# A decoder layer on one core: feed-forward tiles in the gates' order, quantisation spread over two feature tiles, a first unit in groups of three half steps, and own PSUM banks for two projection pieces

## The chip, the core and the metric

The kernel runs on one core of one Trainium2 chip. The metric is the device time of one execution in microseconds (us). The engines are TensorE (PE in the profile; PEld is its loading of weights), VectorE (DVE), ScalarE (ACT), GpSimd (POOL) and SyncE (SP), which issues most of the DMAs. Each of the four compute engines works through its own instructions in order.

## What is computed

Everything is float32. The batch has 4 sequences of 1024 tokens with 512 features. The reference, cut to what matters:

```python
# attention: 32 heads of 16 channels; every projection is two linear layers in a row
q, k, v = (lin(lin(x, w, wb), vw, vb) for each of q, k, v)
o = softmax(q @ k.T / 4) @ v                  # per head, 1024 x 1024 scores
x = layernorm(x + lin(shuffled(o), wo))
# gates: x is taken as (1024 channels, 512 positions); halves h and c, z0 prepended
out = ctx + conv1d(h, weight, kernel 2) + bias    # 2048 output channels
i, o, g, f = split(out, 4)
c = sigmoid(f) * c_before + sigmoid(i) * tanh(g)
x = layernorm(x + concat(sigmoid(o) * tanh(c), c))
# feed-forward: quantised activations, ternary weight
x_dq = clip(round(x / scale), -127, 127) * scale
x = layernorm(x + x_dq @ (ternary_weight - 1).T + bias)
```

## The kernel before

**Set-up (attention, L311-L369).** The two linear layers of q, of k and of v are folded into one weight each. For q and k this takes 16 matmuls of 128 x 128 by 128 x 512 apiece (L358-L363), accumulated in four PSUM banks each and copied out by VectorE (tiles 1 and 3) and ScalarE (tiles 2 and 4) at L364-L368. The pool of these banks has eight one-bank buffers; the first goes to ten matmuls of zeros (`idle`), the next eight to the two folds. At L369 the pool is closed, and at L371 and L372 the attention's two pools are opened: `ps_st` with four one-bank buffers and `ps_nat` with two two-bank buffers, eight banks in all.

**Pieces.** `project` (L393) makes 160 or 176 columns of q or k for eight heads: 16 matmuls of 32 output columns, four of them side by side (`by_quarters`, L53). `qk_pieces` (L427) is the list of six such pieces. `fold_v` (L408), `project_v` (L414) and `out_piece` (L436) are pieces of the same shape for the folding of v, for v and for the projection of the attention's output. Each takes one buffer of `ps_st`.

**Units.** A unit is a sequence and a group of four heads, 32 units in all. `nat` (L444) multiplies q by k for two heads in order to find each row's maximum (a VectorE reduction, L473, or L469 for single tiles); each head uses 32 of the 128 rows of TensorE's array, and `pair` says which two of the four row groups. `scores` (L510) makes the transposed scores for two heads, whose exponentials ScalarE takes (L538); `weigh` (L543) multiplies them by v. In the usual unit the `nat` of the next unit and the `scores` of this one go side by side, 32 half steps per unit (L682). The two ends differ (L648-L680): ahead of the first unit (`u == -1`) there is only `nat`, in 16 steps of two half steps each, the second with two single `ps_st` tiles (`apart`) instead of a `ps_nat` tile; between the steps 25 pieces are spread evenly (the last three of v's fold, six of q, sixteen of v). In the last unit there is only `scores`, with one `out_piece` behind every even step while any is left, which is until step 10. Behind it, one last `weigh` and the start of the second sequence's normalisation close the attention (L725-L736).

**Tail.** Sequences go in two rounds, (0, 2) and then (1, 3). A round has 32 gates: for each of four feature tiles t, for each of the two sequences, for each of four gates g (L987-L990). The conv with two taps is computed for three outputs at a time with four matmul groups per gate (`gate`, L793, L798-L803); the inputs `xf` of these groups are sums and differences made by VectorE (`fir_parts`, L172, L185-L191). VectorE adds each gate's results to the context in four operations (L807, L810, L811, L813), and ScalarE applies the sigmoid or tanh (L814). `pc` and `pa` are the PSUM tiles, two buffers each. After the fourth gate `combine` (L822) makes two token tiles, t and 4 + t, on GpSimd and ScalarE, their statistics (`third`, L842), the square root (`fourth`, L117), the normalisation (`fifth`, L121) and a sum on GpSimd (`sixth`, L856).

`feed_forward` (L922) goes over the 16 token tiles of the round's two sequences. `quantise` (L867) is one ScalarE operation (L871) and two of VectorE (L872, L873); `turn` (L876) transposes on TensorE and copies back on ScalarE (L881); `feed` (L884) multiplies in one of two PSUM buffers, and `residual` (L890) adds and takes statistics (L892, L893). A tile is quantised four tiles ahead; the first four are quantised in the gates, and the first two are turned between the taps of one of the last gates.

**What sets the order.** The order is written by hand. `after(n, work)` (L758) puts work into a list that is due n steps later, and `step()` (L761), called after every gate and every feed-forward tile, issues what is due on whichever engine it needs. The offsets of `combine` are these (L859), for second, third, fourth, fifth and sixth:

```python
        steps = (4, 6, 7, 8, 9) if last else (1, 3, 4, 5, 6)
```

and the order of the feed-forward tiles and the places of quantisation (`place` counts 0 to 7 in the last feature tile alone, L992) are

```python
    order = [t for t in range(NT) if t % 4 < 3] + [3, 7]
...
                    if place in (1, 2, 3, 4):
                        quantise(batches[0], order[place - 1])
```

Of the kernel before, what the change touches and what calls it, by code (L numbers as in the profile page):

```python
# [8 lines left out]
F32 = mybir.dt.float32  # L9
# [3 lines left out]
PSUM = bass.MemoryType.PSUM  # L13

P = 128
# [232 lines left out]
def attention(ctx, tc, a, attn_d, ident, shared, hand):  # L248
# [73 lines left out]
    pt = ps.tile([P, P], F32, tag="ps", name="idle_ps")  # L322
    for n in range(10):
        nc.tensor.matmul(pt, idle, idle, start=True, stop=True)
    for which, (w, v, dst) in enumerate((("wq", "vq", b_q), ("wk", "vk", b_k), ("wv", "vv", None))):
# [38 lines left out]
        for f in range(FT):  # L364
            if f % 2:
                nc.scalar.copy(w_d[:, f, :], pts[f])  # L366
            else:
                nc.vector.tensor_copy(w_d[:, f, :], pts[f])  # L368
    setup_ps.close()  # L369

    ps_st = ctx.enter_context(tc.tile_pool(name="ps_st", bufs=4, space=PSUM))  # L371
    ps_nat = ctx.enter_context(tc.tile_pool(name="ps_nat", bufs=2, space=PSUM))  # L372

    units = [(b, g) for b in range(B) for g in range(NG)]
    NU = len(units)
    QW = 256
# [13 lines left out]

    late_rows = []

    def project(p, which, t0, n, packed):  # L393

        b, gg = divmod(p, 4)
        w, bias = ((w_q, b_q), (w_k, b_k))[which]
        cols = slice(t0, t0 + n)
        pt = ps_st.tile([P, QW], F32, tag="st", name=f"proj{p}_{which}_{t0}")
        by_quarters(nc, pt[:, 0:n], lambda f: w[:, f, gg * P : (gg + 1) * P], lambda f: xts[b][:, f, cols])
        nc.scalar.activation(packed[:, cols], pt[:, 0:n], AF.Identity, bias=bias[:, gg : gg + 1], scale=1.0)  # L400
        if t0 + n == S:
            to_quadrants(2 * p, which, packed)
            if which == 0 and p > 0:
                late_rows.append(lambda: to_quadrants(2 * p + 1, 0, packed))
            else:
                to_quadrants(2 * p + 1, which, packed)

    def fold_v(f, half):  # L408
        cols = slice(half * QW, half * QW + QW)
# [4 lines left out]
    def project_v(b, t, half):  # L414
# [12 lines left out]
    def qk_pieces(p, which):  # L427


        parts = [(0, 176), (176, 176), (352, 176), (528, 176), (704, 160), (864, 160)]  # L430
        return [lambda part=part: project(p, which, *part, packs[:, which, :]) for part in parts]

    def v_pieces(b, t):
        return [lambda half=half: project_v(b, t, half) for half in range(2)]
# [197 lines left out]
    for u in range(-1, NU):  # L632
        fill = []
        if (u + 3) % 2 == 0 and (u + 3) // 2 < NU // 2:
            fill += qk_pieces((u + 3) // 2, 0)
        elif u % 2 == 0 and u // 2 + 1 < NU // 2:
            fill += qk_pieces(u // 2 + 1, 1)
        if u == -1:
            fill = folds[5:] + fill
            fill += [piece for t in range(NT) for piece in v_pieces(0, t)]  # L640
        elif units[u][0] + 1 < B:
            fill += v_pieces(units[u][0] + 1, units[u][1])
        if u == -1:
# [4 lines left out]
        if u == -1 or u + 1 == NU:  # L648
            total, done = len(fill), 0
            for i in range(HS // 2):  # L650
                if u == -1:
                    after = [nat(0, i, 0), nat(0, i, 1, apart=True)]
                else:
                    after = [scores(u, i, i % 2), scores(u, i, 1 - i % 2, wide=True)]
                for work in after:
                    work()
                if i % 2 == 0 and weighing:
                    weigh(*weighing.pop(0))
                if u >= 0 and i % 2 == 1:
# [3 lines left out]
                if u >= 0 and i > 1 and firsts:  # L663
                    firsts.pop(0)()
                if i == 1 and u >= 0:
                    hand.first_w = hand.load_conv(0, None)
                if i in (3, 5) and u >= 0:
                    hand.load_ctx(i // 2 - 1)
                if i in (8, 9, 10, 11) and u >= 0:
                    hand.sum_taps(hand.first_w, i - 8)  # L670
                if i < 2 and u >= 0:
                    shift(u, 1, i == 0)
                if i in (8, 10) and u == -1:
                    shift(0, 0, i == 8)
                if i in (2, 5, 8, 11) and stages:
                    stages.pop(0)()
                until = total * (i + 1) // (HS // 2)
                for piece in fill[done:until]:
                    piece()
                done = until  # L680
        else:
            for h in range(HS):  # L682
                i, half = divmod(h, 2)
                for work in (nat(u + 1, i, half), scores(u, i, 1 - half)):
                    work()
                if h % 4 == 1 and weighing:
                    weigh(*weighing.pop(0))
                if h in (1, 3):
                    shift(u, 1, h == 1)
                if h in (17, 19):  # L690
                    shift(u + 1, 0, h == 17)
                if h == 2 and late_rows:
                    late_rows.pop()()
                if h % 4 == 3:
                    weighing.append((u, h // 4))
                    if fill:
                        fill.pop(0)()
                    elif u > 24 or u == 24 and h > 24:
                        out_pieces.pop(0)()
                if h in (5, 9, 13, 20) and stages:  # L700
                    stages.pop(0)()
                if h == 5 and u == 24:
                    hand.load_w_o()
                    hand.load_attention(0, big_slot(0, "big0"))
                    hand.load_residual(0)
                    hand.load_rest()
                if h == 21 and 25 <= u < 29:
                    hand.prepare_w_f(u - 25)
                if h == 21 and u == 29:
                    hand.prepare_rest()  # L710
                if h == 5 and u == 30:
                    hand.x1[0], firsts = hand.first_norm(0)
                    firsts.pop(0)()
                    hand.xf[0], parts = hand.fir_parts(0, hand.x1[0], shared)
                    firsts.extend(parts)
                if h == 5 and u == 29:
# [22 lines left out]
def tail(ctx, tc, a, out, ident, eps, hand):  # L739
# [18 lines left out]
    def after(steps, work):  # L758
        later.append((now + max(steps, 1), work))
# [59 lines left out]
            scale=1.0,  # L819
        )  # L820

    def combine(b, t, k, last):  # L822


        u, y, x = us[b, t], ys2[b], x1[b]
# [228 lines left out]
```

## Time and profile before

| what | us |
|---|---|
| median of three runs (2443.67 to 2444.45) | 2444.41 |
| the profiled execution | 2444.41 |
| its span, first to last instruction | 2442.6 |
| set-up and first pieces, to 56.7 | 56.7 |
| ahead of the first unit, 56.7 to 117.7 | 61.0 |
| the usual units, 117.7 to 1909 | 1791.3 |
| last unit, to 1951 | 42.0 |
| first round: 32 gates to 2104.2, feed-forward to 2166.8 | 153.2, 62.6 |
| projection of the second round, to 2222 | 55.2 |
| second round: gates to 2373.7, feed-forward and end to 2442.6 | 151.7, 68.9 |

The granted TensorE clock is 0.999 of full speed over the span. A row of the timeline gives start, duration, engine, line and operation, `out<-in`, shapes and count; in brackets stands how long the engine was idle before it and who ended that idle time. A row of waits gives the waiting line, the releaser, and total, number and longest of such waits. One float32 matmul of the program is two matmul instructions in the trace. Matmuls are pipelined, so that the durations of neighbours overlap: what one costs is the distance from its start to the next one's.

### The profile page before, as it was taken

To read this page: it belongs to the slowest core of one execution; us is meant where nothing else is said; L and a number is where in the kernel's file an instruction comes from. 1 tells how busy PE (TensorE), PEld (TensorE's weight loads), DVE (VectorE), ACT (ScalarE), POOL (GpSimd) and SP (SyncE) were. 2 spreads that over 40 slices of the span, in tenths; PEclk is the share of its full clock that TensorE was granted. 3 is DMA by queue.
4 is the path that set the end of the run, shared out by engine and by line. 5 is a ranking of instruction groups with operands and counts; after the bars stand their busy time and mean duration, and the time that the engine had idled before them with its cause. 6 is when DMAs were issued, how large, how long until landed. Compare 5 with 4: busy or idle time off the path is not lost.

```text
span 2442.6 us, 74358 instructions
## 1 busy us (share of the span) xinstructions
PE 2426.3 (99%) x32604; PEld 1692.5 (69%) x32604; DVE 1740.9 (71%) x2181; ACT 1337.1 (55%) x2592; POOL 374.2 (15%) x310
## 2 busy tenths in 40 slices
PE   9999999999999999999999999999999999999998
PEld 5566666666666666666666666666666699647994
DVE  3777777777777777777777777777777476878677
ACT  1066666666666666666666666666655723411342
POOL 2000000000000000000000000200020268322761
PEclk9999999999999999999999999999999999999999
DMA  6101112111111111011111114111120242160301
GB/s 220 50 12 21 21 21 60 21 21 22 24 22 25 30 47 25 19 23 22 21 21 24 23 21 129 27 25 22 26 84 12 81 148 94 61 225 18 121 35 69
DMA packets 80852, 121.70 MB, mean 50 GB/s; under 512 B 39072, under 2 KB 39328, under 8 KB 80528
## 3 DMA queue, kind: packets, MB, share of 16 engines
q1 hardware_dynamic: 79808, 115.77, 17.3%
q8 instruction: 256, 4.19, 0.8%
q10 hardware_dynamic: 720, 1.18, 0.1%
q14 instruction: 68, 0.56, 0.1%
HBM read 80.77 MB, written 18.35 MB: 41 GB/s over the span
## 4 chain that ended last, share of the span: by engine, by line
PE 97%; DVE 2%; ACT 1%; issue 0%; DMA 0%; SPq 0%; DVEq 0%; ACTq 0%
PE nat L457 22%; PE av L553 20%; PE st L527 18%; PE proj L59 10%; PE pc L803 5%; PE pa L803 5%; PE v L59 5%; PE pf L887 4%; PE po L59 2%; PE po L237 2%; PE fold L361 1%; PE fold L59 1%; PE tr L879 1%; DVE u L813 0%; DVE y L121 0%
## 5 line engine op out<-in xcount | busy, mean ns | idle before, releaser
L473 DVE TENSOR_REDUCE mx<-nat 128x2 f32<-128x1024 f32 x1008 | 1187.6, 1219 | 439.0 <-PE st L527 412.0
L538 ACT ACTIVATE at<-st 128x512 f32<-128x512 f32 x2016 | 1042.3, 603 | 607.7 <-PE st L527 595.3
L457 PE MATMUL nat<-qk 32*128 32x512 f32 x4032 | 1012.5, 614 | 0.5 <-DVE mx L473 0.5
L527 PE MATMUL st<-qk 32*128 32x256 f32 x8064 | 997.8, 388 | 0.0
L527 PEld LDWEIGHTS st<-qk 32*128 32x128 f32 x8064 | 663.1, 184 | 44.9 <-issue 3.7
L553 PE MATMUL av<-at,v_sb 128*32 128x256 f32 x8192 | 498.5, 382 | 1.5 <-ACT at L538 1.5
L457 PEld LDWEIGHTS nat<-qk 32*128 32x128 f32 x4032 | 343.7, 184 | 188.2 <-DVE mx L473 119.7
L553 PEld LDWEIGHTS av<-at,v_sb 128*32 128x32 f32 x8192 | 241.4, 110 | 223.1 <-ACT at L538 92.2
L600 POOL TENSOR_TENSOR o_n<-o_sb,rbc 128x512 f32<-128x512 f32 x64 | 97.1, 1538 | 1672.4 <-DMA rbc<-rec_d 1488.0
L59 PE MATMUL proj<-xT,w_qk 128*32 128x176 f32 (+1 forms) x6144 | 259.4, 311 | 0.7 <-ACT w_qk L366 0.7
L59 PEld LDWEIGHTS proj<-xT,w_qk 128*32 128x32 f32 x6144 | 181.7, 110 | 81.5 <-ACT at L538 59.9
L803 PE MATMUL pc<-xf,w 128*128 128x171 f32 x1024 | 160.1, 308 | 4.6 <-DVE u L807 4.0
L803 PE MATMUL pa<-xf,w 128*128 128x171 f32 x1024 | 159.8, 308 | 0.0
L803 PEld LDWEIGHTS pc<-xf,w 128*128 128x128 f32 x1024 | 151.9, 189 | 6.3 <-DVE u L807 4.8
L803 PEld LDWEIGHTS pa<-xf,w 128*128 128x128 f32 x1024 | 152.1, 189 | 0.0
L814 ACT ACTIVATE u<-u,b_c 128x512 f32<-128x512 f32 x64 | 46.3, 723 | 167.3 <-DVE u L813 166.3
L59 PE MATMUL v<-w_v,xT 128*32 128x256 f32 x2048 | 122.5, 382 | 0.0
L887 PE MATMUL pf<-w_f,xq_t 128*128 128x512 f32 (+1 forms) x264 | 115.2, 581 | 1.7 <-ACT xq_t L881 1.7
L566 DVE TENSOR_TENSOR o_sb<-av,o_sb 128x256 f32<-128x256 f32 x128 | 54.3, 424 | 71.5 <-PE av L553 70.9
L59 PEld LDWEIGHTS v<-w_v,xT 128*32 128x32 f32 x2048 | 60.8, 110 | 58.0 <-ACT at L538 16.5
L170 POOL TENSOR_TENSOR w<-w 128x512 f32<-128x512 f32 x64 | 81.0, 1298 | 100.3 <-DMA w<-in_conv_wT 56.6
L564 ACT COPY o_sb<-av 128x256 f32<-128x256 f32 x128 | 48.0, 375 | 77.9 <-PE av L553 59.3
(99 smaller groups left out, 1325.7 us busy)
## 6 DMA issues: line engine op xcount, KB each, us to landing
qk<-qk SPq DMA_DIRECT2D x256, 64.0 KB
w<-in_conv_wT SPq DMA_DIRECT2D x32, 512.0 KB
u<-in_ctx SPq DMA_DIRECT2D x16, 1024.0 KB
xT<-in_xT SPq DMA_DIRECT2D x16, 512.0 KB
rbc<-rec_d SPq DMA_DIRECT2D x128, 64.0 KB
attn<-o_n SPq DMA_DIRECT2D x256, 32.0 KB
big<-attn SPq DMA_DIRECT2D x4, 2048.0 KB
y<-in_x SPq DMA_DIRECT2D x4, 2048.0 KB
```

Of the source, the lines that this page charges most:

```text
L59: nc.tensor.matmul(pt[r, :], lhsT(f)[:, r], rhs(f), start=f == 0, stop=f == FT - 1)
L170: self.nc.gpsimd.tensor_tensor(w[:, i, tap, :], w[:, i, 0, :], w[:, i, 1, :], op)
L237: nc.tensor.matmul(pt, attn_t[:, f, t * P : (t + 1) * P], self.w_o[:, f, cols], start=f == 0, stop=f == FT - 1)
L457: nc.tensor.matmul(pts[n], q_ts[u % 4][r : r + 32, qt * P : (qt + 1) * P], k_ts[u % 4][r : r + 32, kh * 512 : kh * 512 + 512], start=True, ...
L473: nc.vector.tensor_reduce(mxs[u][:, qt, 2 * pair : 2 * pair + 2, kh], pt, AX.X, ALU.max, negate=True)
L527: nc.tensor.matmul(st[:, k * QW : k * QW + QW], k_ts[u % 4][r : r + 32, kt * P : (kt + 1) * P], q_ts[u % 4][r : r + 32, qq * QW : qq * QW ...
L538: nc.scalar.activation(at, st, AF.Exp, scale=0.25)
L553: nc.tensor.matmul(av[32 * j : 32 * j + 32, :], v_sb[b % 2][:, kt, c * VW : c * VW + 32], ats[u, 2 * i + n // 2, j][:, n % 2 * QW : n % 2 ...
L566: nc.vector.tensor_add(o, av, o)
L600: nc.gpsimd.tensor_mul(o_n[:, :, half * 256 : half * 256 + 256], o_sb[:, cols].rearrange("p (s e) -> p e s", e=2), rbc[:, cols].rearrange( ...
L803: nc.tensor.matmul(pt, w[:, i, tap, o : o + P], xf[:, tap, i, :], start=i == 0, stop=i == FT - 1)
L887: nc.tensor.matmul(pt, xq_ts[b, t][:, f, :], hand.w_f[:, f, cols], start=f == 0, stop=f == FT - 1)
```

## The change

It has six edits.

1. The tiles of the feed-forward are taken in the order 0, 4, 1, 5, 2, 6, 3, 7, in which the gates finish them, instead of 0, 1, 2, 4, 5, 6, 3, 7.
2. `place` counts the gates 0 to 31 over all four feature tiles. The first four tiles are quantised behind gates 18, 20, 22 and 25; the old places 1 to 4 are gates 25 to 28. The place of the two first turns (30) stays. For the next-to-last `combine` (behind gate 27) the fourth, fifth and sixth parts come 6, 7 and 8 steps later instead of 4, 5 and 6.
3. The two parts of the second sequence's `fir_parts` at the start of the tail come behind the second and third gate instead of the first and second.
4. Ahead of the first unit, `nat` goes in eleven groups of three half steps (the last has two), and the 25 pieces are spread behind these. The two `shift` DMAs move to groups 6 and 7.
5. In the last unit one `out_piece` is kept back; it is issued behind the last scores and ahead of the last `weigh`.
6. The pool of the set-up has six PSUM banks, and a new pool `early_ps` two. The zeros and the first two pieces of q use `early_ps`; these two pieces are issued ahead of the closing of the set-up's pools, the rest as before.

```diff
-    ps = setup_ps.enter_context(tc.tile_pool(name="setup_ps", bufs=8, space=PSUM))
+    ps = setup_ps.enter_context(tc.tile_pool(name="setup_ps", bufs=6, space=PSUM))
+    early_ps = setup_ps.enter_context(tc.tile_pool(name="early_ps", bufs=2, space=PSUM))
...
+    early = qk_pieces(0, 0)
+    for piece in early[:2]:
+        piece(early_ps)
+    setup_ps.close()
+
+    ps_st = ctx.enter_context(tc.tile_pool(name="ps_st", bufs=4, space=PSUM))
+    ps_nat = ctx.enter_context(tc.tile_pool(name="ps_nat", bufs=2, space=PSUM))
...
-    for piece in qk_pieces(0, 0) + qk_pieces(0, 1) + folds[:5]:
+    for piece in early[2:] + qk_pieces(0, 1) + folds[:5]:
...
+        if u == -1:
+            total, done, steps = len(fill), 0, HS // 3 + 1
+            for n in range(steps):
+                hs = range(3 * n, min(3 * n + 3, HS))
+                for work in [nat(0, h // 2, h % 2, apart=h % 2 == 1) for h in hs]:
+                    work()
+                if n in (6, 7):
+                    shift(0, 0, n == 6)
+                until = total * (n + 1) // steps
+                for piece in fill[done:until]:
+                    piece()
+                done = until
...
-                if u >= 0 and i % 2 == 0 and out_pieces:
+                if i % 2 == 0 and len(out_pieces) > 1:
                     out_pieces.pop(0)()
...
+    out_pieces.pop()()
     assert not out_pieces
     while weighing:
         weigh(*weighing.pop(0))
...
-        steps = (4, 6, 7, 8, 9) if last else (1, 3, 4, 5, 6)
+        steps = (4, 6, 7, 8, 9) if last else (1, 3, 6, 7, 8) if next_to_last else (1, 3, 4, 5, 6)
...
-    order = [t for t in range(NT) if t % 4 < 3] + [3, 7]
+    order = [t // 2 + t % 2 * 4 for t in range(NT)]
...
-        after(m + 1, part)
+        after(m + 2, part)
...
-                    place = 4 * (b == batches[1]) + g if t == 3 else 0
-                    gate(b, t, g, w, (lambda: [turn(batches[0], order[m]) for m in (0, 1)]) if place == 6 else None)
+                    place = 8 * t + 4 * (b == batches[1]) + g
+                    gate(b, t, g, w, (lambda: [turn(batches[0], order[m]) for m in (0, 1)]) if place == 30 else None)
                     if g == 3:
-                        combine(b, t, k, place == 7)
-                    if place in (1, 2, 3, 4):
-                        quantise(batches[0], order[place - 1])
+                        combine(b, t, k, place == 31, place == 27)
+                    if place in (18, 20, 22, 25):
+                        quantise(batches[0], order[(place - 18) // 2])
```

More of the change, by code (lines that the diff above doesn't have):

```diff
@@ L317, in attention @@
     setup_ps = ExitStack()
-    ps = setup_ps.enter_context(tc.tile_pool(name="setup_ps", bufs=8, space=PSUM))
+    ps = setup_ps.enter_context(tc.tile_pool(name="setup_ps", bufs=6, space=PSUM))
+    early_ps = setup_ps.enter_context(tc.tile_pool(name="early_ps", bufs=2, space=PSUM))
     idle = sp.tile([P, P], F32, tag="idle", bufs=1, name="idle")
     nc.vector.memset(idle, 0.0)
-    pt = ps.tile([P, P], F32, tag="ps", name="idle_ps")
+    pt = early_ps.tile([P, P], F32, tag="ps", name="idle_ps")
     for n in range(10):
@@ L368, in attention @@
                 nc.vector.tensor_copy(w_d[:, f, :], pts[f])
-    setup_ps.close()
-    ps_st = ctx.enter_context(tc.tile_pool(name="ps_st", bufs=4, space=PSUM))
-    ps_nat = ctx.enter_context(tc.tile_pool(name="ps_nat", bufs=2, space=PSUM))
     units = [(b, g) for b in range(B) for g in range(NG)]
@@ L391, in attention, with project @@
     late_rows = []
-    def project(p, which, t0, n, packed):
+    def project(p, which, t0, n, packed, pool=None):
         b, gg = divmod(p, 4)
@@ L397, in project @@
         cols = slice(t0, t0 + n)
-        pt = ps_st.tile([P, QW], F32, tag="st", name=f"proj{p}_{which}_{t0}")
+        pt = (pool or ps_st).tile([P, QW], F32, tag="ps" if pool else "st", name=f"proj{p}_{which}_{t0}")
         by_quarters(nc, pt[:, 0:n], lambda f: w[:, f, gg * P : (gg + 1) * P], lambda f: xts[b][:, f, cols])
@@ L406, in project, with qk_pieces @@
                 to_quadrants(2 * p + 1, which, packed)
+    def qk_pieces(p, which):
+        parts = [(0, 176), (176, 176), (352, 176), (528, 176), (704, 160), (864, 160)]
+        return [lambda pool=None, part=part: project(p, which, *part, packs[:, which, :], pool) for part in parts]
+    early = qk_pieces(0, 0)
[4 more added lines that the diff above has]
+    ps_nat = ctx.enter_context(tc.tile_pool(name="ps_nat", bufs=2, space=PSUM))
     def fold_v(f, half):
@@ L425, in project_v @@
         )
-    def qk_pieces(p, which):
-        parts = [(0, 176), (176, 176), (352, 176), (528, 176), (704, 160), (864, 160)]
-        return [lambda part=part: project(p, which, *part, packs[:, which, :]) for part in parts]
     def v_pieces(b, t):
@@ L646, in attention @@
             xts[units[u][0] + 2] = load_x(units[u][0] + 2)
-        if u == -1 or u + 1 == NU:
-            total, done = len(fill), 0
-            for i in range(HS // 2):
[L651 to L655, printed above, removed]
+        if u == -1:
[10 more added lines that the diff above has]
+                done = until
+        elif u + 1 == NU:
+            assert not fill
+            for i in range(HS // 2):
+                for work in [scores(u, i, i % 2), scores(u, i, 1 - i % 2, wide=True)]:
                     work()
@@ L658, in attention @@
                     weigh(*weighing.pop(0))
-                if u >= 0 and i % 2 == 1:
+                if i % 2 == 1:
                     weighing.append((u, i // 2))
-                if u >= 0 and i % 2 == 0 and out_pieces:
+                if i % 2 == 0 and len(out_pieces) > 1:
                     out_pieces.pop(0)()
-                if u >= 0 and i > 1 and firsts:
+                if i > 1 and firsts:
                     firsts.pop(0)()
-                if i == 1 and u >= 0:
+                if i == 1:
                     hand.first_w = hand.load_conv(0, None)
-                if i in (3, 5) and u >= 0:
+                if i in (3, 5):
                     hand.load_ctx(i // 2 - 1)
-                if i in (8, 9, 10, 11) and u >= 0:
+                if i in (8, 9, 10, 11):
                     hand.sum_taps(hand.first_w, i - 8)
-                if i < 2 and u >= 0:
+                if i < 2:
                     shift(u, 1, i == 0)
-                if i in (8, 10) and u == -1:
-                    shift(0, 0, i == 8)
                 if i in (2, 5, 8, 11) and stages:
                     stages.pop(0)()
[L677 to L680, printed above, removed]
         else:
@@ L820, in gate, with combine @@
         )
-    def combine(b, t, k, last):
+    def combine(b, t, k, last, next_to_last):
         u, y, x = us[b, t], ys2[b], x1[b]
```

## The prediction

> **What bounds the kernel now.** I read the page's busy shares first, then TensorE's waits, then the gaps between matmuls (from their times in the trace), then the timeline around each gap.
>
> ```profile
> span 2442.6 us, 74358 instructions
> PE 2426.3 (99%) x32604; PEld 1692.5 (69%) x32604; DVE 1740.9 (71%) x2181; ACT 1337.1 (55%) x2592; POOL 374.2 (15%) x310
> ```
>
> TensorE is the bound: 16.3 us of the span have no matmul, and 6.3 of these lie behind the last one (it ends at 2436.3). So about 10 us are to be had as gaps, besides stalls that hide inside "busy" because matmuls overlap. The change doesn't alter the number of matmuls. TensorE's waits name the gaps (total, times, longest):
>
> ```profile
> PE pc L803 <- DVE u L807: 4.0, 3, 1.7
> PE pf L887 <- ACT xq_t L881: 1.7, 4, 0.6
> PE av L553 <- ACT at L538: 1.5, 2, 0.9
> PE proj L59 <- ACT w_qk L366: 0.7, 1, 0.7
> PE pc L803 <- DVE o_sb L566: 0.6, 1, 0.6
> ```
>
> The first row is one gap of 1.7 in each round of gates (at 2093.9 and 2363.4) and one of 0.57 at 1965.9. The second is 0.64 at 2112.7 and 0.63 at 2382.3 (and twice 0.2 later). The third holds 0.63 at 1948.9, the fourth stands at 34.1. The other 0.9 of the third row (1915.4, early in the last unit) and a 0.48 in unit 0 are not touched.
>
> **1. Quantising over two feature tiles, feed-forward order (two rounds).** I number the gates of a round 0 to 31; one takes TensorE 4.67 us. Before, the first four tiles are quantised behind gates 25 to 28. The timeline at the gap:
>
> ```profile
> 2087.52 0.80 ACT L871 ACTIVATE xq<-y,magic,sc 128x512 f32<-128x512 f32 x1
> 2088.35 0.90 DVE L872 TENSOR_SCALAR xq<-xq 128x512 f32<-128x512 f32 x1 [1.50 <-ACT xq L871]
> 2089.28 1.38 DVE L873 TENSOR_SCALAR xq<-xq,sc 128x512 f32<-128x512 f32 x1
> 2090.77 2.52 DVE L121 TENSOR_SCALAR y<-y,mv,rstd 128x512 f32<-128x512 f32 x2
> 2093.22 0.61 DVE L807 TENSOR_TENSOR u<-pc,u 128x342 f32<-128x342 f32 x1
> 2093.88 2.60 PE L803 MATMUL pc<-xf,w 128*128 128x171 f32 x16 [1.71 <-DVE u L807]
> ```
>
> VectorE stands 1.50 for ScalarE's half of the quantisation, does its own 0.43 + 0.49 (0.90 + 1.38 while GpSimd works beside it), then the normalisation, and only then frees the PSUM bank that the gate two further on needs. A gate costs VectorE about 2.5 (0.63 + 0.63 + 0.39 + 0.87), a quantisation 2.4 to 3.8, statistics of a pair of tiles 1.6, a normalisation 1.2 to 2.7. Gates 25 to 28: 4 x 2.5 + 4 x 3.1 + 2 x 1.6 + 2 x 1.9 = 29 against 4 x 4.67 = 18.7; two banks carry the rest until they are out by 1.7.
>
> After, the quantisations are behind gates 18, 20, 22 and 25. Gates 18 to 25: 8 x 2.5 + 4 x 3.1 + 2 x 1.6 + 2 x 1.9 = 39 against 37.4. Gate by gate, slow durations wherever GpSimd is busy (its tap sums fill 2057.3 to 2064.8), VectorE finishes gate 20 at 2052.7, 22 at 2062, 24 at 2073.5, 25 at 2076, the last about when it did before. A gate stalls TensorE only if VectorE finishes it later than some 6.5 after its last matmul (1.9 is normal); the worst, gate 24, ends 4.8 after. So no stall takes its place, and the gaps of 1.71 and 1.69 go.
>
> The same lateness makes the gap at the third feed-forward tile: it waits for its PSUM buffer, freed by L892 of the first tile, whose row ends at 2382.12 just ahead of it (ScalarE's copy, which the profile names, ended later, but is the next tile's). With gates 26 to 31 free of quantisations, and the square root with its table loads moved from gate 31 to behind the first feed-forward tile, VectorE is done with gate 31 1.9 after its end, ScalarE's next quantisation lies at +2.7 to +3.5, VectorE's part ends by +5.8, L892 by +6.5; the third tile starts at 2 x 3.87 = +7.7. Gone: 0.64 + 0.63.
>
> Behind the moved square root the copy for the third tile waits on ScalarE. The rows give load 1.28 + root 0.30 back to back (2352.70, 2354.00), with the reload due only at the next tanh: +3.5 + 1.6 + 0.6 = +5.7, in time for +7.7. The Trainium skill (ScalarE: Activation LUTs, What ACT_TABLE_LOAD costs) speaks against the move: it adds a drain and counts 2.66 for each switch. No such drain stands between these rows. By the rule the copy would end at +7.1, so the cover shrinks from 2.0 to 0.6; the sum is nought by both, and I take the row. If the cover failed, each further us would cost twice, once a round.
>
> The third unknown is the normalisation of tiles 3 and 7, now behind the second tile's feed: the quantisation of tile 3 waits for it, and behind that the copies for later tiles. By the same sum it ends near +10, the fourth tile starts at +11.6. Zero. The changed order itself, the same instructions on other tiles, costs zero. Part 1: **-4.7** (bounds -4.9 and -2.3).
>
> **2. Out-projection kept back.** At the end of the last unit the last weighing waits for its exponentials:
>
> ```profile
> 1948.24 1.09 ACT L538 ACTIVATE at<-stw 128x512 f32<-128x512 f32 x2
> 1948.90 1.55 PE L553 MATMUL av<-at,v_sb 128*32 128x256 f32 x16 [0.63 <-ACT at L538]
> ```
>
> The weighing runs from 1947.2 to about 1950.3, 3.1, where 32 such matmuls take 1.73 (8 x 0.216): 1.35 of stall. One piece of 1.72 now stands ahead of it. It is missing at step 10, where ScalarE (8 exponentials of 0.477 in each pair of steps, 3.8) is nearly the bound: pairs without the piece take 4.28 instead of 3.8. ScalarE had 1.71 idle there and uses it up; following slots and exponentials through steps 11 to 15, the weighing ends at 1948.6: -1.65. VectorE's add and statistics of that piece (0.42 + 0.69) fall into the weighing; the first gate still waits its 0.6 for the last sum. Taken **-1.65** (-1.3 to -2.3).
>
> **3. FIR of batch 2 one gate later.** At 1965.24 VectorE reaches L807 only after L185 and L186 (2.32 + 2.41, slow beside GpSimd); TensorE waits 0.57. With gate 1's four operations ahead, that bank is free near 1961.4. The FIR then runs near 1963.1 to 1965.9, gate 2's operations to 1968.3, the second part to 1970.4; batch 2 needs it at 1971.0. Margin 0.6: **-0.57** (bounds -0.57 and 0).
>
> **4. Own banks for two pieces.** The projection's 0.68 is a wait for the last copy of the second fold (33.43 + 0.58). Its first two pieces need only w_q, so they follow the fold at once. But the folds have six banks instead of eight: tiles 3 and 4 of the second fold take banks of the first. Its third tile's matmul stands at 21.2 (weights at 20.79, one instruction earlier), and VectorE's first copy (L368, from 20.76, 0.68) frees the bank at 21.44: 0.28 of new wait, on TensorE, with the whole second fold behind it. **-0.4** (bounds -0.75, if the bank copied by ScalarE at 18 is given first, and +0.3, if the pieces wait nonetheless).
>
> **5. Three half steps at a time in the first unit.** The view is TensorE's timeline:
>
> ```profile
> 66.93 0.70 PE L457 MATMUL nat<-qk 32*128 32x512 f32 x2
> 66.94 0.69 PE L457 MATMUL nats<-qk 32*128 32x512 f32 x1
> ...
> 67.47 1.22 PE L457 MATMUL nats<-qk 32*128 32x512 f32 x3
> 68.63 2.59 PE L59 MATMUL proj<-xT,w_qk 128*32 128x176 f32 x64
> ...
> 90.99 1.94 PE L59 MATMUL v<-w_v,xT 128*32 128x256 f32 x32
> 92.86 0.70 PE L457 MATMUL nat<-qk 32*128 32x512 f32 x2
> ```
>
> nat and nats stand side by side: a half step uses two of the four row groups, and two half steps run in the time of one, 2 x 0.43 = 0.86. A step with one value piece repeats after 2.94 (97.61 to 100.55 is another), with two after 4.66, so a piece is 1.72 and the step's own part 1.22: 0.86 + 0.36 for changing to 32-row matmuls and back. Sum of 16 steps: 19.5; pieces 3 x 1.72 + 4 x 1.18 + 2 x 1.08 + 16 x 1.72 = 39.6; together 59.1. The unit takes 60.9 (56.73 to 117.66), so 1.8 is waiting for PSUM, of which two of 0.6 (67.47 shows one).
>
> After: eleven changes instead of sixteen, but a third half step uses the same row groups as the first and starts when they are free: 2 x 0.86 + 0.36 = 2.08. Ten times this + 1.22 = 22.0, +2.5. The Trainium skill (TensorEngine Tiling (Array Packing), Key Properties) says that changing the tiling mode drains the array: that counts the changes alone, 5 x 0.36 = 1.8 gained. The same trace shows the streams that the rule leaves out, so I take the row. Of the 1.8 waiting, about 0.6 stays: a batch with four single tiles holds all four banks, and the next piece gets one at some 2.0 to 2.1, when the first of VectorE's reductions (0.68) is through. Part 5: 22.0 + 39.6 + 0.6 - 60.9 = **+1.2** (+0.6 to +2.5). The two shifts of this unit come a few us later, with over 30 us to the scores that read them.
>
> **Sum.** -4.7 - 1.65 - 0.57 - 0.4 + 1.2 = -6.1. The profiled execution took 2444.41, 1.8 more than its span, and is the median of the three runs: 2444.4 - 6.1 = **2438.3**.
>
> **Rivals.** (a) *The stall moves with the quantisation.* At gates 18 to 22 GpSimd's sums slow VectorE, and half of part 1 comes back: 2438.3 + 2.3 = 2440.6, within 0.2%. For: 0.90 + 1.38 beside GpSimd, 39 against 37.4. Against: two banks of room. (b) *The three half steps pay, as the drain rule has it*: -1.8 and no PSUM waits, -3.6 in place of +1.2: 2433.5. Against: the row groups. (c) *Slower.* In the first unit, each of the five batches with four single tiles has its next piece wait for all its reductions: 1.3 + 1.1 + 4 x 0.6 = 4.8 after its start, not 2.1: 5 x 2.7 = 13.5, 2451.8. It turns the sign from 6.1 / 5 = 1.2 for each such batch, and counts as slower from 2.2. Against: banks are freed one by one, and VectorE has 4.3 of work in 5.5. (d) *Nothing measurable*: each queue hides its part elsewhere, 2444.
>
> **Chances.** Forecast 0.64, (a) 0.20, (b) 0.08, (c) 0.05, (d) 0.03. A difference of 0.2%, 4.9 us, is about what can be told from none. Of the forecast's 0.64 some 0.06 lies above 2439.5, of (a) 0.04 below: faster 0.70, same 0.25, slower 0.05. The range takes the bounds of parts 2, 4 and 5 and case (a): 2436.2 to 2441.9; outside stay (b), (c) and a few per cent of the rest.
>
> **What would show it.** Gaps ahead of pc in both rounds and ahead of the third pf gone; the last weighing in 1.8 without a wait; pc at 1965.9 without one; a wait of about 0.3 inside the second fold and none ahead of proj; the first unit's half-step batches 2.1 long, the unit 1 longer. Wrong it would be if VectorE still frees a gate's bank late, or if the first unit got shorter.

## The result, and the profile after

The changed kernel takes 2439.24 us (median of 12 runs, 2438.01 to 2440.08) where the kernel before takes 2444.43 beside it: a ratio of 0.9979, with a 95% interval of 0.9970 to 0.9988. The forecast was 2438.3, in a range of 2436.2 to 2441.9. The profiled execution took 2438.52, 5.9 less than the profiled one of before. The head of its page, the span and the busy shares:

```profile
span 2436.7 us, 74361 instructions
PE 2425.8 (100%) x32604; PEld 1694.4 (70%) x32604; DVE 1742.6 (72%) x2181; ACT 1336.2 (55%) x2592; POOL 374.6 (15%) x310
```

The number of matmuls is the same and so is TensorE's busy time, to 0.5 us: what was gained are gaps. TensorE's waits of the changed kernel (total, times, longest):

```profile
PE pf L895 <- ACT xq_t L889: 1.5, 2, 0.8
PE idle_ps L325 <- DVE idle L322: 1.0, 1, 1.0
PE av L557 <- ACT at L542: 0.9, 1, 0.9
PE pc L811 <- DVE o_sb L570: 0.6, 1, 0.6
PE nat L461 <- DVE mx L477: 0.5, 1, 0.5
```

Of the four waits that the forecast wanted gone, three are: `pc <- DVE u` (4.0), `proj <- ACT w_qk` (0.7), and the 0.63 of the last weighing (`av` now has only the early 0.9). The 0.6 of `pc <- o_sb` and the 0.5 of `nat` were expected to stay. But the row of the feed-forward, `pf <- ACT xq_t`, has hardly moved: 1.7 in four waits became 1.5 in two.

To see where the time went, I cut both spans at the same matmuls (first `fold`, first `nat`, first `pc`, and so on) and subtracted:

| stage | before | after | difference |
|---|---|---|---|
| start, to the first fold | 5.48 | 5.26 | -0.22 |
| the two folds, to the first `proj` | 28.59 | 27.56 | -1.03 |
| ahead of the first unit (first `nat` to first `st`) | 60.94 | 61.54 | +0.60 |
| usual units | 1784.00 | 1784.87 | +0.87 |
| last unit with its last weighing, to the first gate | 49.38 | 48.07 | -1.31 |
| first four gates of the first round | 19.62 | 18.77 | -0.85 |
| the other 28 gates of the first round | 133.52 | 131.54 | -1.98 |
| feed-forward of the first round | 62.44 | 62.39 | -0.05 |
| gates of the second round | 152.16 | 150.21 | -1.95 |
| feed-forward of the second round | 62.61 | 62.60 | -0.01 |
| behind the last matmul | 6.28 | 6.31 | +0.03 |

The sum is -5.9. Two stages that are alike to 0.01 (22.66 from the first `proj` to the first `nat`, and the projection of the second round, 54.93) are left out. The last unit begins here with its first `stw`, at 1901.67 in the profile of before, and not at the 1909 of the table further up. Two of these rows are no part of the change: the first row, which lay between 4.79 and 5.48 in the profiles of all fourteen kernels, and the usual units, which lay between 1783.95 and 1784.87, whatever was edited (the last section shows why). The folds took 28.31 to 28.37 in the four experiments that leave the set-up alone, so that 0.28 of the -1.03 belongs to the one profile of before.

### The profile page after: what moved, and what is told of

It reads as the page before. It is cut to its first block, busy times and chain, and to the rows that moved or that the text cites. A ratio compares the mean times of both kernels' runs of the same rounds, so it can differ in the third digit from the quotient of the medians.

```text
span 2436.7 us, 74361 instructions
## 1 busy us (share of the span) xinstructions
PE 2425.8 (100%) x32604; PEld 1694.4 (70%) x32604; DVE 1742.6 (72%) x2181; ACT 1336.2 (55%) x2592; POOL 374.6 (15%) x310
## 4 chain that ended last, share of the span: by engine, by line
PE 99%; DVE 0%; ACT 0%; issue 0%; DVEq 0%; ACTq 0%
PE nat L461 22%; PE av L557 20%; PE st L531 18%; PE proj L59 10%; PE pc L811 6%; PE pa L811 6%; PE v L59 5%; PE pf L895 4%; PE po L59 2%; PE po L237 2%; PE fold L362 1%; PE fold L59 1%; PE tr L887 1%; PE nats L461 0%; PE idle_ps L325 0%; PE stw L531 0%
```

## The experiments

All twelve were timed in five rounds beside the kernel before, which was at 2443.75 to 2444.51 in the four series. The intervals of single runs reach about 2 us to either side. So small parts are read from the stages of the profiles, and the medians stand beside them. Where the code is the same, a stage repeats to 0.1 us, except for the start, the folds, the usual units and the first unit in groups of three or four (56.3 to 56.9 with four), of which several profiles have to be taken together.

### The rounds alone

Edits 1 and 2 put into the kernel before: the order, the places and the later steps.

```diff
-    order = [t for t in range(NT) if t % 4 < 3] + [3, 7]
+    order = [t // 2 + t % 2 * 4 for t in range(NT)]
...
+        steps = (4, 6, 7, 8, 9) if last else (1, 3, 6, 7, 8) if next_to_last else (1, 3, 4, 5, 6)
...
+                    if place in (18, 20, 22, 25):
+                        quantise(batches[0], order[(place - 18) // 2])
```

> The kernel before with edits 1 and 2 alone (feed-forward order, places of quantisation, later steps of the next-to-last combine). Theory, as read from the profile after: the gates' gap goes and brings 2.0 a round, the third tile's gap goes too, but its 0.8 is given back at the tenth tile, where ScalarE stands on a square root; so -4.0 (2440.4), with a gap of about 0.8 ahead of the tenth pf in each round. Rival, the forecast as it stands: both gaps are gained, -4.7 (2439.7). Rival, the stall moves to gates 18 to 25: -2.3 or less (2442).

Measured: 2440.5, ratio 0.9984 (0.9977 to 0.9990). Both rounds of gates have the changed kernel's length to 0.01 us (131.54 and 150.21), and the feed-forwards keep that of before (62.41, 62.59), with the same 0.78 ahead of the tenth tile. So this part is worth 4.0, all of it from the gates, and none of the other edits takes a share in it.

### Three half steps alone, none, and four

Edit 4 alone in the kernel before (the new branch for `u == -1`):

> The kernel before with edit 4 alone (first unit in groups of three half steps). Theory (row groups): the third half step shares its two row groups with the first, a group takes 2 x 0.86 + 0.36, the unit 61.5 instead of 60.9 with no wait for PSUM left: +0.6 (2445.0). Rival (only the changes of tiling mode count): five changes fewer and no PSUM waits, the unit 57.3: -3.6 (2440.8).

Measured: 2445.43, ratio 1.0004 (0.9996 to 1.0012); the stage takes 62.26 instead of 60.94, +1.32. In the changed kernel, the other way about, the edit undone:

```diff
-            total, done, steps = len(fill), 0, HS // 3 + 1
+            total, done, steps = len(fill), 0, HS // 2
...
-                hs = range(3 * n, min(3 * n + 3, HS))
+                hs = range(2 * n, 2 * n + 2)
...
-                if n in (6, 7):
+                if n in (8, 10):
...
```

> The changed kernel with the first unit again in sixteen steps of two half steps. Theory (row groups): -0.6 against the changed kernel, 2438.6, within what five rounds can hardly tell; the profile decides: the unit at 60.9 with PSUM waits of 1.8, against 61.5. Rival (the three half steps help elsewhere, by an emptier VectorE at the start of the usual units): slower than the changed kernel by 1 or more.

Measured: 2437.95, ratio 0.9973 (0.9964 to 0.9983), 1.3 below the changed kernel; the stage is back at 60.95. Over the five profiles with groups of three the stage takes 61.54 to 62.73, 62.0 in the mean; the two longest hold a gap of 0.74 and of 0.41 ahead of a projection piece, for which the trace names no cause. Alone or in company, the edit makes the stage longer by about 1 us; the ratio of the run with the edit alone can't be told from 1.

If two half steps side by side are one pass, then a fourth costs nothing that the third hasn't paid. So, in the changed kernel, eight groups of four, in an order in which the two that use the same rows are not neighbours (two lines further up, which prepare and finish the maxima of a row, follow that order and are left out here):

```diff
-            total, done, steps = len(fill), 0, HS // 3 + 1
+            total, done, steps = len(fill), 0, HS // 4
...
-                hs = range(3 * n, min(3 * n + 3, HS))
+                hs = [4 * n + d for d in (1, 0, 3, 2)]
...
-                if n in (6, 7):
+                if n in (4, 5):
...
```

> The changed kernel with the first unit in eight groups of four half steps, in the order 1, 0, 3, 2 of each four, so that single tiles are reduced first and two pairs of half steps fill all four row groups. Theory (row groups): 8 x (2 x 0.86 + 0.36) + 39.6 = 56.2 instead of 61.5: -5.3 against the changed kernel, 2434. Rival (mode changes alone): three changes fewer, -1.1, 2438.1. Rival (PSUM): four single tiles hold all four banks, the pieces behind wait about 1 in each group, and the gain is 5 smaller or gone: 2439 or above.

Measured: 2433.2, ratio 0.9954 (0.9942 to 0.9967); the stage takes 56.93, 5 less than that mean. TensorE's timeline shows why. First the changed kernel, one group of three and the value piece behind it, up to the next group:

```profile
81.37 0.70 PE L461 MATMUL nats<-qk 32*128 32x512 f32 x2
...
81.92 0.59 PE L461 MATMUL nat<-qk 32*128 32x512 f32 x2
82.33 1.02 PE L461 MATMUL nats<-qk 32*128 32x512 f32 x4
83.28 3.66 PE L59 MATMUL v<-w_v,xT 128*32 128x256 f32 x64
86.88 0.70 PE L461 MATMUL nat<-qk 32*128 32x512 f32 x2
```

Up to 82.33 `nat` and `nats` stand in pairs; then `nats` stands alone, four instructions at 0.43 behind one another, in a pass whose other half is empty. The piece starts 1.91 after the group. The same view of a group of four:

```profile
69.20 0.70 PE L461 MATMUL nats<-qk 32*128 32x512 f32 x2
...
70.59 0.59 PE L461 MATMUL nats<-qk 32*128 32x512 f32 x2
70.61 0.59 PE L461 MATMUL nat<-qk 32*128 32x512 f32 x2
71.13 3.60 PE L59 MATMUL proj<-xT,w_qk 128*32 128x176 f32 x96
```

It is in pairs to the end, and the piece behind it starts after 1.93: four half steps in the time of three.

### The out-projection, the FIR and the banks, each alone

Three kernels with one edit each in the kernel before.

```diff
-                if u >= 0 and i % 2 == 0 and out_pieces:
+                if u >= 0 and i % 2 == 0 and len(out_pieces) > 1:
...
+    out_pieces.pop()()
```

> The kernel before with edit 5 alone (one out-projection piece kept back for the end of the last unit). Forecast: -1.65. Theory from the profile after: -1.3, the length of the last weighing's stall, because without its piece at step 10 the last unit is bound by ScalarE's exponentials from there on and the slack gives nothing more (2443.1). Rival (ScalarE binds wholly, the piece only moves): 0, 2444.4.

```diff
-        after(m + 1, part)
+        after(m + 2, part)
```

> The kernel before with edit 3 alone (the second sequence's FIR one gate later). Forecast: -0.57. Theory from the profile after: -0.85, the gap and the slower first matmuls behind it (2443.6). Rival: it shows only together with edit 5, and the gap turns up at the second sequence's first gate, 0 (2444.4). Five rounds hardly tell these; the profile's gap and the start of the first gates do.

The third has edit 6 as the change has it:

```diff
-    ps = setup_ps.enter_context(tc.tile_pool(name="setup_ps", bufs=8, space=PSUM))
+    ps = setup_ps.enter_context(tc.tile_pool(name="setup_ps", bufs=6, space=PSUM))
+    early_ps = setup_ps.enter_context(tc.tile_pool(name="early_ps", bufs=2, space=PSUM))
...
+    for piece in early[:2]:
+        piece(early_ps)
+    setup_ps.close()
```

> The kernel before with edit 6 alone (own banks for two projection pieces). Forecast: -0.4, as the gap of 0.68 ahead of proj goes and a wait of about 0.3 comes up in the second fold. Theory now: -0.7 when the bias weights land early and VectorE's copy is through in time, -0.4 when they don't; between 2443.7 and 2444.1. The profile shows which: a gap of 0.3 inside the second fold, or none.

Measured, with stages in the order out-projection, FIR, banks: 2443.17 (0.9995, 0.9987 to 1.0003), 2443.27 (0.9996, 0.9988 to 1.0004), 2443.65 (0.9997, 0.9989 to 1.0005), against 2444.43. Each interval by itself holds 1. The stages don't leave it open: the last unit 48.07 instead of 49.38, the first four gates 18.77 instead of 19.62, the folds 27.56 instead of 28.31. The lengths are those of the changed kernel, so each edit does the whole of its part and needs no other.

### The feed-forward: steps, root and places

Here was the open question: the gap at the third tile is gone, yet the stage is as long as it was. In the changed kernel the gap stands at the tenth tile (timeline of all engines):

```profile
2131.09 0.60 PE L887 MATMUL tr<-ident,xq 128*128 128x128 f32 x4
...
2135.12 0.36 DVE L911 BATCH_NORM_AGGREGATE mv<-stats 128x2 f32<-128x6 f32 x4
2135.51 0.30 ACT L117 ACTIVATE rstd<-mv,eps 128x4 f32<-128x4 f32 x1 [6.30 <-DVE mv L911]
2135.72 0.56 ACT L889 COPY xq_t<-tr 128x512 f32<-128x512 f32 x1
...
2136.33 3.70 PE L895 MATMUL pf<-w_f,xq_t 128*128 128x512 f32 x8 [0.77 <-ACT xq_t L889]
```

The copy that feeds the tenth tile was ready at 2131.7, when its transpose ended. It starts at 2135.72, because ahead of it in ScalarE's queue stands the square root for the last norm of the fifth to the eighth tile (L117), which waits 6.30 for VectorE's variances (L911), and these stand behind VectorE's last work on the eighth tile. The profile names the copy; the wait is VectorE's. At the sixth tile the root of the first four tiles does the same on a smaller scale:

```profile
2118.99 0.30 ACT L117 ACTIVATE rstd<-mv,eps 128x4 f32<-128x4 f32 x1 [3.49 <-DVE mv L911]
2119.19 0.56 ACT L889 COPY xq_t<-tr 128x512 f32<-128x512 f32 x1
```

The kernel before had the root in that place too, and lost less by it, at the tenth tile alone:

```profile
2139.48 0.30 ACT L117 ACTIVATE rstd<-mv,eps 128x4 f32<-128x4 f32 x1 [5.75 <-DVE mv L903]
...
2140.30 3.27 PE L887 MATMUL pf<-w_f,xq_t 128*128 128x512 f32 x7 [0.22 <-ACT xq_t L881]
```

My first suspect was edit 2's later steps, which bring a normalisation of two tiles (1.2 us of VectorE, L118 and L121 from 2109.49) into the feed-forward. The changed kernel with the steps of before:

```diff
-        steps = (4, 6, 7, 8, 9) if last else (1, 3, 6, 7, 8) if next_to_last else (1, 3, 4, 5, 6)
+        steps = (4, 6, 7, 8, 9) if last else (1, 3, 4, 5, 6)
```

> The changed kernel with the next-to-last combine's old steps (square root at gate 31 again). Theory (what is gained at the third tile is given back at the tenth, where VectorE and the square root set the time): the gap of about 0.6 or less at the third pf is back, the one at the tenth is smaller by as much, and the time is that of the changed kernel, 2439.2. Rival (forecast): the gap at the third tile costs its 0.64 in each round, 2440.5.

Measured: 2437.25, ratio 0.9971 (0.9959 to 0.9982): lower than either expectation, and 2.0 below the changed kernel. The feed-forwards take 61.52 and 61.71, 0.9 less each, with 0.18 left of the gap:

```profile
2135.47 0.30 ACT L117 ACTIVATE rstd<-mv,eps 128x4 f32<-128x4 f32 x1 [5.71 <-DVE mv L911]
...
2136.30 1.98 PE L895 MATMUL pf<-w_f,xq_t 128*128 128x512 f32 x4 [0.18 <-ACT xq_t L889]
```

So the later steps, of which I had forecast that they cost nothing, cost 0.9 in each round. Nor were they needed for the third tile: it takes 3.87 in this run too, so that with the new places its gap stays away wherever the square root stands.

Next the queue itself: the steps as the change has them, but the variances and the root of a group of four issued one tile later, behind the next tile's copy.

```diff
-        closing = []
+        closing, roots = [], []
...
                 turn(tiles[k + 1][0], tiles[k + 1][2])
+            while roots:
+                roots.pop()()
...
-                first()
+                if group == 4:
+                    roots.append(first)
+                else:
+                    first()
...
-                    after(1, invert)
+                    after(2, invert)
...
-                        after(1 + m, part)
+                        after(2 + m, part)
```

> The changed kernel, but the statistics and the square root of a group of four feed-forward tiles are issued one tile later, behind the next turn, so that the copy of the turned tile does not stand behind the square root on ScalarE; the group's normalisations are one step later too. Theory (ScalarE's order): the gap of 0.77 ahead of the tenth pf goes in both rounds, with the 0.1 to 0.2 at the fifth and sixth tile: -1.5 to -2 against the changed kernel, 2437.4. Rival (VectorE binds there): the tenth or eleventh pf waits for its PSUM buffer instead, and the time stays at 2439.2.

Measured: 2436.3, ratio 0.9967 (0.9954 to 0.9979), 2.9 below the changed kernel, by the stages 2.0: the feed-forwards take 61.08 and 61.26, 1.3 less each, and their tiles follow at 3.87 without a gap; behind the last matmul stands 7.00 instead of 6.31, since the last sequence's own group came later too. At the tenth tile:

```profile
2131.70 0.59 ACT L889 COPY xq_t<-tr 128x512 f32<-128x512 f32 x1 [2.58 <-PE tr L887]
...
2135.31 3.17 PE L895 MATMUL pf<-w_f,xq_t 128*128 128x512 f32 x7
...
2135.90 0.30 ACT L117 ACTIVATE rstd<-mv,eps 128x4 f32<-128x4 f32 x1 [3.62 <-DVE mv L911]
```

The copy goes as soon as its transpose ends, and the root, no earlier than before, waits behind it and holds up nobody.

The last piece of it: the quantisations put back to the old places, with the order and the later steps kept.

```diff
-                    if place in (18, 20, 22, 25):
-                        quantise(batches[0], order[(place - 18) // 2])
+                    if place in (25, 26, 27, 28):
+                        quantise(batches[0], order[place - 25])
```

> The changed kernel with the quantisations behind gates 25 to 28 again (new order and later steps kept). Theory: the gates' gap of 1.7 is back in each round; what VectorE then lacks is paid once, so the tenth tile's gap of 0.77 is smaller or gone: +2 to +4, 2441 to 2443. Rival (the later steps of the next-to-last combine were what removed the gap): the gap stays away, 2439.2.

Measured: 2444.31, ratio 1.0000 (0.9992 to 1.0008), and not 2441 to 2443. The gates' gaps are back (1.67 and 1.69), as expected, but the feed-forwards are longer instead of shorter, 63.26 and 63.37. The tenth tile's gap is still there, and the sixth tile's small loss has become a second gap, behind the root of the first four tiles:

```profile
2122.57 1.98 PE L895 MATMUL pf<-w_f,xq_t 128*128 128x512 f32 x4 [0.87 <-ACT xq_t L889]
```

Set side by side, these runs settle the question. Time from the first product of the first feed-forward to the tenth tile's, 34.83 if nothing is late (9 x 3.87):

| | steps of before | later steps |
|---|---|---|
| old places | 36.11 (before) | 36.93 |
| new places | 35.19 | 36.06 (after) |

The new places bring it forward by 0.9, the later steps put it back by 0.8 to 0.9. With the root out of the way it is 34.84, later steps or not. (The kernel before also has the old order of tiles; that this has no part in its 36.11 was not tried by itself.)

### Both, and the best version

Four half steps and the later root together:

> The changed kernel with both: four half steps in a group and the square root behind the next turn. If the two are independent, 2433.2 and what the square root's run gains, 2431.5. If VectorE binds in the feed-forward, 2433.2.

Measured: 2431.6, ratio 0.9948 (0.9935 to 0.9960); first unit 56.31, feed-forwards 61.08 and 61.26. The two add up: 2433.2 less the 2.0 of the stages is 2431.2. In the last kernel the steps of before came back too, and the roots are moved only in a round's first sequence:

```diff
-                if group == 4:
+                if group == 4 and not last:
...
-                    after(2, invert)
+                    after(1 + (not last), invert)
...
```

> The changed kernel with four half steps at a time in the first unit, the earlier order of the next-to-last combination's later steps (1, 3, 4, 5, 6), and the variance and root of a group of four issued a tile later only in a round's first sequence, so that the last sequence's end stays as it was. Theory (the two edits to the feed-forward take away the same wait of ScalarE's copy behind the root, and the root's place is the better of them): each round's feed-forward 61.1 in place of 62.5, end 6.3, and 2433.2 - 2 x 1.36 = 2430.5 us; no gap over 0.1 us before a product of the feed-forward. Rival (the earlier order sets it whatever the root does: 61.5 a round, with a gap of about 0.2 at the tenth tile): 2433.2 - 2 x 0.9 = 2431.4. Third (the root's group of the last sequence was the one that mattered, and leaving it in place brings the wait back): 2432 or more.

Measured: 2430.98, ratio 0.9947 (0.9934 to 0.9961). The first round's feed-forward takes 61.08 and the second's 61.26, as with the root alone, and the end is 6.29. So the rival is out, and so is the third: the steps have nothing left to do once the root is moved, and only the first sequence's groups mattered. From the time of the previous version this can't be told, and the 0.5 between the measured time and the theory's 2430.5 is within what the runs spread. TensorE's waits:

```profile
PE idle_ps L325 <- DVE idle L322: 1.1, 1, 1.1
PE av L557 <- ACT at L542: 0.9, 1, 0.9
PE pc L811 <- DVE o_sb L570: 0.6, 1, 0.6
PE nat L461 <- DVE mx L477: 0.5, 1, 0.5
```

No row of the feed-forward is among its waits any more. This version beats both kernels: 12.8 us below the one before, about 8 below the change.

## Why the prediction was right, point by point

**Gates: right, a little too small.** Forecast 1.71 + 1.69 gone; measured 1.98 + 1.95, because besides the gap some stall hid in matmuls that overlap. No stall took its place. Behind the quantisation of gate 22, slow beside GpSimd as assumed:

```profile
2063.10 1.37 DVE L881 TENSOR_SCALAR xq<-xq,sc 128x512 f32<-128x512 f32 x1
...
2064.39 0.62 DVE L815 TENSOR_TENSOR u<-pc,u 128x342 f32<-128x342 f32 x1
...
2066.73 1.47 PE L811 MATMUL pc<-xf,w 128*128 128x171 f32 x9
```

L815 frees its bank at 2065.01 and the gate that takes it starts at 2066.73, with 1.7 to spare. Rival (a), the stall moving with the quantisation, is refuted there.

**Third feed-forward tile: this step failed.** "Gone: 0.64 + 0.63" holds of the gap and not of the time. By the distance from one transpose to the next, the third tile took 4.75 before and takes 3.87 now, so even 0.88 went; but the sixth took 3.87 and takes 4.15, and the tenth 4.36 and now 4.91: 0.28 + 0.55 given back, and 0.05 is left. What had been wrong was the nought for the moved normalisation of tiles 3 and 7. I followed it up to the fourth tile, where it does no harm, and not to the next instructions that make another engine wait for VectorE, the variances of each group of four tiles. The moved square root with its table load, on which I had weighed the rule, was not the trouble:

```profile
2103.75 1.28 ACT L117 ACT_TABLE_LOAD   x1
2105.04 0.30 ACT L117 ACTIVATE rstd<-mv,eps 128x2 f32<-128x2 f32 x1
2105.25 0.56 ACT L889 COPY xq_t<-tr 128x512 f32<-128x512 f32 x1
```

Load and root stand back to back again, and the copy for the third tile ends 5.54 after the first product (2100.27), where I had summed 5.7 by the rows and 7.1 by the rule. A root that waits on VectorE was the trouble, with the copy behind it. The part came to 4.0 instead of 4.7, inside its bounds (2.3 to 4.9). Of the 2.7 that the two feed-forwards can give (to 61.08 and 61.26), the change takes next to none.

**Out-projection: right, 1.31 instead of 1.65.** The end of the last unit in the changed kernel:

```profile
1945.68 1.93 PE L59 MATMUL po<-w_o,big 128*32 128x256 f32 x32
...
1947.44 1.91 PE L557 MATMUL av<-at,v_sb 128*32 128x256 f32 x32
```

The weighing is one run of 32 matmuls without a wait, 1.91 against about 3.1. The stall of 1.35 went as named; the further 0.3, which I had booked from following ScalarE's slots ahead of it, did not come; why was not tried.

**FIR: right, 0.85 instead of 0.57.** No gap is left; as with the gates, the gap was less than the stall.

**Banks: right, with the wait depending on the execution.** The folds came down by 0.75 against the 28.31 that is usual without the edit. The 0.28 that I had put into the second fold is not in this profile; it is in that of the version with four half steps, to the hundredth almost and at the matmul named:

```profile
20.81 1.98 PE L362 MATMUL fold<-v_t,w_n 128*128 128x512 f32 x4 [0.29 <-DVE w_qk L369]
```

There VectorE's first copy (L369) starts at 20.07, in the changed kernel's profile at 19.81. The stage is 28.12 with that wait. Over the nine profiles with the edit it takes 27.56 to 28.42, 27.84 in the mean, and over the five without 28.38: -0.5, near the -0.4.

**Three half steps: right in sign and cause.** Forecast +1.2 (its own terms, 22.0 + 39.6 + 0.6 - 60.9, make 1.3); measured +0.6 in the changed kernel's profile, +1.1 in the mean of five, about 1 in the medians. Rival (b), which took the rule that a change of the tiling mode drains the array (the Trainium skill, TensorEngine Tiling (Array Packing), Key Properties) for the whole of the price, gave -3.6 for this edit and is refuted by the run with this edit alone. With the row groups filled, the stage does get shorter, by 4.0 against two half steps (60.94 to 56.93). Eight changes fewer at the forecast's 0.36 would make 2.9 of it; the rest, waits for PSUM by the forecast's sum, was not taken apart. Rival (c), slower by PSUM tiles, would have made the stage 13.5 longer than the forecast and did not come.

**The sum.** The forecast was -6.1; the stages of the change give -0.75 + 0.6 - 1.3 - 0.85 - 2.0 - 1.95 - 0.05 = -6.3, the profiled executions differ by 5.9 and the medians by 5.2. The total is nearer than its parts: what the third tile didn't give (1.2) was made up by the gates (0.5), the FIR (0.3), the banks (0.35) and the cheaper half steps (0.6), less 0.35 of the out-projection. That is partly luck. With the means of several profiles for the folds (-0.5) and the first unit (+1.1) the stages give -5.6, near the 5.2 of the medians.

## What to carry to other kernels

When a gap closes and its stage stays as long, look for the next instruction in the same queue that waits for the same engine; here a tiny square root, issued early, stood between a finished transpose and its copy. An engine that works in order should get the operation whose input is late behind those whose input is there, even if it then starts later. And count passes through the array before counting changes of mode: three half steps cost as much as four.

## What I had not expected of the hardware

A VectorE operation of 128 x 16 elements, 0.19 us in the median, took this at one place of the usual units in the changed kernel, beside a sum of GpSimd's:

```profile
1809.66 1.32 DVE L483 TENSOR_TENSOR neg<-mx 128x16 f32<-128x16 f32 x1
```

```profile
1808.42 3.75 POOL L100 TENSOR_TENSOR y<-y,b_o 128x512 f32<-128x512 f32 x3
```

The same operation took 0.53 there in the profile of before (1810.23). Between the matmuls on either side of it the two traces drift apart by 0.8, most of the 0.9 by which they differ in the usual units. In the profile of the rounds alone it took 1.08 at the same place.

The fourteen profiles together say more. In each of them this operation begins 1692.6 after the first `st`, to 0.05, while GpSimd's sums of 1.26 to 1.30 apiece lie differently. In thirteen of them it is over 0.04 to 0.05 after the end of the sum that was running when it began, however long that was: here after 1.32, in the profile of before after 0.53, and elsewhere after 0.23 to 1.33. In the fourteenth (the FIR alone) the sum ended 0.12 after the operation's start, and the operation took its ordinary 0.19. The usual units grow with it: 1783.95 where it took 0.19 or 0.23, 1784.00 at 0.53, 1784.37 at 0.82, 1784.68 at 1.13, 1784.87 at 1.32. So most of the 0.87 in the table comes from where a GpSimd sum happened to lie. That VectorE waits there for GpSimd's instruction to end is read from these times; no run took the sum away. Each kernel has one profile, so it isn't known whether the place of the sum changes between executions of the same kernel. A single profile can't tell less than 1 us in that stage.
